# A sparse graph-attention layer: weight loads ordered behind attention's first work, degrees and target rows kept in a small table, the second sort's scatters spaced wider

## The chip, the cores and the metric

The kernel runs on one core of a Trainium2 chip. The metric is the device time of one execution in microseconds (us). Before the change three runs took 1833.16, 1834.15 and 1836.34 us; the median is 1834.15 us.

## The reference

The inputs are x and h_target (4096 nodes, 512 features each), an adjacency matrix adj (4096 x 4096 integers, about 0.4% of them nonzero, the diagonal always set), a node mask that is all ones, and weights in float32. The layer is masked attention with 8 heads of 64, a feed-forward part with hidden size 2048, two residuals and a last normalisation:

```
hs = layer_norm(x);  ht = layer_norm(h_target)
q = (ht @ Wq + bq) / sqrt(64);  k = hs @ Wk + bk;  v = hs @ Wv + bv
logits = einsum('thd,shd->hts', q, k);  logits = where(adj != 0, logits, -1e30)
ctx  = einsum('hts,shd->thd', softmax(logits), v)
ht   = layer_norm(ht + ctx @ Wo + bo)
out  = _layernorm(x + ht + gelu(ht @ W1) @ W2)
```

A row of adj has some 10 to 40 nonzeros (its degree), so most of the 4096 x 4096 logits are never needed.

## The kernel before

The kernel does the attention sparsely. It goes through these stages, which overlap.

**Lists.** For each of 32 tiles of 128 target rows, `edges` (L716) loads four quarters of adj (512 KB each, on SyncE's DMA queue, SP), takes the sign of each entry on ScalarE (L728), and finds the column numbers of the nonzeros with VectorE's maximum operations (L733 to L756). The candidates of each tile that go beyond the first 24 are kept by a write to DRAM, `rest_d` (L766, on SP); the buffer `gid` that this write reads has only one copy, so the next tile's L747 on VectorE waits until the write has landed. The result for a target row is a record: its degree (`DEG`, word 0), its own row number (`TGT`, word 1), two numbers for its first normalisation, and up to 40 column numbers.

**Sort.** The rows are sorted by degree, in two parts of 16 tiles, so that each tile of 128 sorted rows has a tight cap on its degree (`CAPS_A`, `CAPS_B`). `sort(part)` (L807) computes ranks and then writes the records to DRAM (`recs_d`) with 16 indirect scatters on GpSimd's queue (L853).

**Projections.** `project` (L864) goes through x in 16 groups of two tiles and computes k and v; `source` (L919) copies the two products out of PSUM on ScalarE (L931) and stores a tile's k|v rows (512 KB) to the DRAM table `kvd` by ScalarE's DMA queue (L935). A gather of k|v may name any source row, so the first gather has to wait until the last of these stores has landed.

**Attention.** Sorted tile by sorted tile, `attention` (L1164) processes segments of up to three neighbours per target row. GpSimd gathers the k|v rows by record (L966 within `issue`, L1055; 512 KB a gather, one slot of the buffer `ring` each; up to five segments ahead). VectorE multiplies by q and sums (L1217, L1222), ScalarE takes the exponential, and the values are weighted, two neighbours by VectorE (L1181) and the third by ScalarE in `by_scalar` (L1196; eight multiplications, L1201). TensorE adds the weighted values up, transposed, in PSUM (L1189). A tile's front (`front`, L982) gathers its h_target rows by `TGT` (L966), normalises them (L994 on VectorE, L995 on ScalarE), transposes (L999) and computes q (L1008). L994 takes a value of the last k|v copy, of the last segment's logits later on, as an operand, only in order to set its place in the order. `finish` (L1074) divides by the softmax's sum, applies Wo and the second normalisation.

**Feed-forward.** `feed` (L1310) handles one group of one or two tiles: hidden products (L1325), gelu (L1328), output products (L1334). Halfway it gathers the group's x rows into `xt` by `TGT` (L1352); `end` (L1276) adds, normalises and scatters the finished rows to `out` by `TGT` (L1302). W1 and W2 come in quarters. The first two are loaded early on SP, the last two (4 loads of 1 MB) by `weights` (L1436) on ScalarE's queue, into memory that the projections have used (`pools`, L1432).

**Buffers and checks.** A record lies in on-chip memory in one of 7 buffers `rec` (L977). It is read by the front, by the k|v gathers, in `finish`, and last by the x gather and the output scatter, so that its buffer comes free when the output scatter has landed. `verdict` (L1249), traced after the last tile, checks the softmax sums and the degrees. It reads the degrees of all rows back from `recs_d` by two DMAs on SP (L1259), one 4-byte word per row, into `degs`, and compares them with the caps on VectorE (L1262, L1265).

**Order.** The Python code weaves generators: `_weave` (L400) takes a step from the stream whose planned time is smallest, and each `yield` gives the planned time of the step. In the last weave there are four streams:

```
_weave((att, 0), (chain(feed(g) for g in range(len(GROUPS))), 0), (other_lists(), WAIT),
       (weights(), 0))
```

`weights` traces the third quarter at its planned time 10 and the fourth at 20. A segment of the first attention tile takes about 8 units of planned time. The traced order gives priorities. A planner then builds each engine's fixed instruction order: an instruction that is ready earlier in its model may go ahead of earlier traced ones. On the chip each engine and each DMA queue's issuing engine runs its instructions strictly in that order, so one that waits holds up everything behind it. Buffers and waits are derived from the tiles that instructions touch.

Of the kernel before, what the change touches and what calls it, by code (L numbers as in the profile page):

```python
# [443 lines left out]
def adj_resnorm_kernel(  # L444
# [88 lines left out]
    with tc.tile_pool(name="keep", bufs=1) as keep:  # L533
# [10 lines left out]
        cols = keep.tile([P, 5 * KC], F32, name="cols")  # L544
        s1c, b1c, s2c, b2c, bvc = (cols[:, i * KC:(i + 1) * KC] for i in range(5))
        sums = keep.tile([P, NT, H], F32, name="sums")
        degs = keep.tile([P, NT, 1], I32, name="degs")
        bad = keep.tile([P, 8], F32, name="bad")
        nc.vector.memset(bad, 0.0)

        with ExitStack() as late:
# [255 lines left out]
            def sort(part):  # L807
# [44 lines left out]
                for i in range(n):  # L852
                    ins = nc.gpsimd.indirect_dma_start(  # L853
                        out=recs_d[part][:, :],
                        out_offset=bass.IndirectOffsetOnAxis(ap=ranki[:, i:i + 1], axis=0),
                        in_=R[:, i, :], in_offset=None)

                    tc.declare_no_dep(ins.ins, group=f"scatter{part}", reason="other rows")
                    tc.add_to_no_dep_group(f"scatter{part}", ins.ins)
                    yield 1.3  # L860
                done.add(part)


            def project(order, t=None):  # L864
# [54 lines left out]
                def source(n, j):  # L919
                    g, hT = order[n], state[n][1]  # L920
                    if asked or moms:
                        kvr = sp.tile([P, 2 * D], F32, name="tq", bufs=3)
                    else:

                        kvr = ring[:, 8 + (n * G + j) % 3, :]
                    for half, w in enumerate((wk, wv)):
                        pkv = psi.tile([P, D], F32, name="pq", bufs=3)
                        for kc in range(KC):
                            nc.tensor.matmul(pkv, hT[:, kc, j * P:(j + 1) * P], w[:, kc, :],  # L929
                                             start=kc == 0, stop=kc == KC - 1)  # L930
                        nc.scalar.copy(kvr[:, half * D:(half + 1) * D], pkv)  # L931
                    if n >= 14:
                        latest[:] = [kvr[:, 0:1]]
                    r0 = 1 + (g * G + j) * P
                    nc.scalar.dma_start(kvd[r0:r0 + P, :], kvr)  # L935
                    return 7.8

                with tc.manual_schedule(engines={mybir.EngineType.DVE}):
# [21 lines left out]
                        yield cost  # L960


            recs, tqs, h2Ts, done, ready, latest = {}, {}, {}, set(), [], []

            def gather(dst, table, idx):
                nc.gpsimd.indirect_dma_start(  # L966
# [3 lines left out]
            def prefetch(i):  # L970
                if i >= NT or i in recs:
                    return
                r0 = TILES[i][0]
                part = 1 if r0 >= PARTS[1][0] * P else 0
                assert part in done
                r0 -= PARTS[part][0] * P
                rec = sp.tile([P, E0 + MAXE], I32, name="rec", bufs=7)  # L977

                nc.gpsimd.dma_start(rec[:, :RW], recs_d[part][r0:r0 + P, :])
                recs[i] = rec  # L980

            def front(i, idle=0):  # L982


                rec = recs[i]
                tq = sp.tile([P, 2 * D], F32, name="tq", bufs=3)
                t = tq[:, :D]
                gather(t, h_target, rec[:, TGT:TGT + 1])
                for _ in range(1 + idle):
                    yield  # L990


                m = rec[:, RST:RST + 2].bitcast(F32)
                nc.vector.scalar_tensor_tensor(m, m, latest[-1], m, op0=ALU.bypass, op1=ALU.max)  # L994
                nc.scalar.activation(t, t, AF.Identity, bias=m[:, 1:2], scale=m[:, 0:1])  # L995
                yield
                pt = ps.tile([P, KC, P], F32, name="t", bufs=2)
                for kc in range(KC):
                    nc.tensor.transpose(pt[:, kc, :], t[:, kc * P:(kc + 1) * P], ident)  # L999
                hT = tq[:, D:].rearrange("p (c t) -> p c t", c=KC)  # L1000
                for kc in range(KC):
                    nc.scalar.activation(hT[:, kc, :], pt[:, kc, :], AF.Identity,  # L1002
                                         bias=b1r[:, kc:kc + 1], scale=s1c[:, kc:kc + 1])
                yield
                yield
                pq = ps.tile([P, D], F32, name="t", bufs=2)
                for kc in range(KC):
# [156 lines left out]
            def attention():  # L1164
# [31 lines left out]
                def by_scalar(kv, lg):  # L1196
                    pa = sp.tile([P, H], F32, name="pa")
                    nc.scalar.activation(pa, lg[:, S - 1, :], AF.Exp)  # L1198
                    for hd in range(H):
                        v = kv[:, S - 1, D + hd * HD:D + (hd + 1) * HD]  # L1200
                        nc.scalar.mul(v, v, pa[:, hd:hd + 1])  # L1201

                request(0)
                yield 0.0
# [44 lines left out]
            def verdict():  # L1249
# [5 lines left out]
                nc.vector.scalar_tensor_tensor(ok, sf, SUM_HI, ok, op0=ALU.is_lt, op1=ALU.mult)  # L1255
                nc.vector.tensor_reduce(bad[:, 3:4], ok, AX.X, ALU.min)
                nc.vector.tensor_scalar(bad[:, 3:4], bad[:, 3:4], 1.0, None, op0=ALU.not_equal)
                for (i0, n), rec in zip(PARTS, recs_d):
                    nc.sync.dma_start(degs[:, i0:i0 + n, :], rec.rearrange("(n p) w -> p n w", p=P)  # L1259
                                      [:, :, DEG:DEG + 1])  # L1260
                for i, cap in enumerate(CAPS_A + CAPS_B):
                    nc.vector.tensor_scalar(over[:, i:i + 1], degs[:, i, :], float(cap),  # L1262
                                            None, op0=ALU.is_gt)
                nc.vector.tensor_reduce(bad[:, 4:5], over, AX.X, ALU.max)
                nc.vector.tensor_scalar(over, degs[:, :, 0], 1.0, None, op0=ALU.is_lt)  # L1265
                nc.vector.tensor_reduce(bad[:, 5:6], over, AX.X, ALU.max)
                b1 = sp.tile([P, 1], BF16, name="b1", bufs=1)
                nc.vector.tensor_reduce(b1, bad, AX.X, ALU.max)
# [7 lines left out]
            def end(group, xs, po):  # L1276
# [24 lines left out]
                for j, i in enumerate(group):  # L1301
                    ins = nc.gpsimd.indirect_dma_start(  # L1302
                        out=out[:, :], out_offset=bass.IndirectOffsetOnAxis(
                            ap=recs[i][:, TGT:TGT + 1], axis=0),
                        in_=xs[j], in_offset=None)

                    tc.declare_no_dep(ins.ins, group="out", reason="other rows")
                    tc.add_to_no_dep_group("out", ins.ins)

            def feed(g):  # L1310
# [34 lines left out]
                for f0 in range(fb, FC, fb):  # L1345
# [3 lines left out]
                    if f0 == FC // 2:  # L1349
                        for i in group:  # L1350
                            xt = sp.tile([P, D], F32, name="xt")
                            gather(xt, x, recs[i][:, TGT:TGT + 1])  # L1352
                            xs.append(xt)
                    if f0 == fb:

# [80 lines left out]
            def weights():  # L1436


                for q, pool in enumerate(pools):
                    yield 10.0  # L1440
                    load_quarter(pool, q + 2, nc.scalar)

            def other_lists():
                for cost in ed:
# [41 lines left out]
```

## Time and profile before

| | |
|---|---|
| runs | 1833.16, 1834.15, 1836.34 us; median 1834.15 |
| profiled execution | span 1826.4 us from the first to the last instruction, 22937 instructions |
| TensorE (PE) busy | 1687.8 us, 92% |
| VectorE (DVE) busy | 1432.2 us, 78% |
| ScalarE (ACT) busy | 1222.0 us, 67% |
| GpSimd (POOL) busy | 973.8 us, 53% |
| DMA | 463.27 MB, mean 254 GB/s |
| mean granted TensorE clock | 0.963 of full speed |

The profile describes one execution. Its time outside the span is not given; the median of the runs lies 7.75 us above the span. Line numbers (L966) are those of the kernel's file. "Idle before" is the time in which an engine had nothing running just before an instruction; the arrow names what ended it. SPq and ACTq are the DMA issues of SyncE and ScalarE. A share of busy time is a mean over stages with different limits, so the stretches of time count for more than the totals.

### The profile page before, as it was taken

The numbers are of one execution on the slowest core, as the hardware profiler recorded it, in microseconds if no ns is written. First come the engines' busy times: TensorE is split into PE (matmuls) and PEld (weight loads), VectorE is DVE, ScalarE is ACT, GpSimd is POOL, SyncE is SP. The second block draws the span as 40 slices with busy tenths as digits, with TensorE's granted clock in tenths as the row PEclk, the third lists the DMA queues.
The fourth block names the chain that finished last, engine by engine and source line by source line (L and its number), as shares of the span: only waits on it lengthen the run. The fifth ranks groups of instructions, "written<-read, shape, count | busy, mean of one in ns | idle before, by whom it ended". The sixth has DMA issues, their size and how long they took to land. (4 is left out here: it accounts for less than half of the span.)

```text
span 1826.4 us, 22937 instructions
## 1 busy us (share of the span) xinstructions
PE 1687.8 (92%) x7030; PEld 1102.5 (60%) x7030; DVE 1432.2 (78%) x2628; ACT 1222.0 (67%) x3119; POOL 973.8 (53%) x834
## 2 busy tenths in 40 slices
PE   7989983698998989999998998999999999999997
PEld 3444431475666656767676666666666666667664
DVE  6999855999999838786967998999888797988200
ACT  5767634487987637676767777778777676787311
POOL 1000143746566477657567778877574656763101
PEclk9999996698999999999998999999999999999999
DMA  9999958988896648767769978787776767674000
GB/s 354 373 395 365 341 192 309 360 291 312 286 331 231 209 121 312 245 239 260 261 211 308 308 245 302 252 296 265 240 272 222 256 214 262 228 269 159 17 7 25
DMA packets 144396, 463.27 MB, mean 254 GB/s; under 512 B 20628, under 2 KB 25800, under 8 KB 144264
## 3 DMA queue, kind: packets, MB, share of 16 engines
q0 software_dynamic: 96656, 342.64, 54.7%
q1 hardware_dynamic: 39792, 96.00, 14.6%
q10 hardware_dynamic: 7816, 23.08, 3.3%
q8 instruction: 58, 0.95, 0.2%
q14 instruction: 74, 0.61, 0.1%
HBM read 430.76 MB, written 30.89 MB: 253 GB/s over the span
## 5 line engine op out<-in xcount | busy, mean ns | idle before, releaser
L966 POOL DMA_INDIRECT kv<-kvd,rec x603 | 751.4, 1246 | 376.2 <-PE cps L1189 161.4
L1334 PE MATMUL po<-w,gt 128*128 128x512 f32 x1024 | 464.9, 597 | 6.2 <-ACT gt L1328 6.0
L1325 PE MATMUL pf<-h2T,w 128*128 128x256 f32 (+1 forms) x2176 | 464.8, 367 | 0.3 <-ACT h2T L1143 0.3
L1325 PEld LDWEIGHTS pf<-h2T,w 128*128 128x128 f32 x2176 | 388.1, 190 | 64.6 <-issue 20.7
L1217 DVE TENSOR_TENSOR kv<-kv,tq 128x1536 f32<-128x1536 f32 (+2 forms) x211 | 351.7, 1675 | 88.1 <-DMA kv<-kvd,rec 82.9
L1201 ACT ACTIVATE kv<-kv,pa 128x64 f32<-128x64 f32 x1520 | 391.2, 336 | 4.4
L1222 DVE TENSOR_REDUCE lg<-kv 128x24 f32<-128x1536 f32 (+2 forms) x211 | 350.0, 1666 | 1.0 <-ACT pa L1198 0.2
L1189 PE MATMUL cps<-ident,kv 128*128 128x128 f32 x2008 | 269.0, 283 | 53.4 <-issue 23.5
L1189 PEld LDWEIGHTS cps<-ident,kv 128*128 128x128 f32 x2008 | 243.3, 147 | 122.4 <-issue 68.9
L1334 PEld LDWEIGHTS po<-w,gt 128*128 128x128 f32 x1024 | 188.6, 192 | 202.4 <-issue 195.5
L1181 DVE TENSOR_TENSOR kv<-kv,p 128x1024 f32<-128x1024 f32 (+1 forms) x211 | 250.9, 1193 | 23.8 <-ACT p L1226 20.3
L687 POOL TENSOR_TENSOR n_rs<-n_ve,mhalf 128x2 f32<-128x2 f32 (+2 forms) x51 | 46.4, 909 | 336.9 <-DVE n_ve L680 177.7
L728 ACT ACTIVATE kv<-kv 128x1024 uint8<-128x1024 int32 x128 | 134.8, 1054 | 77.1 <-DMA kv<-in_adj_dram 43.3
L1328 ACT ACTIVATE gt<-pf 128x512 f32<-128x512 f32 x128 | 76.3, 597 | 99.2 <-PE pf L1325 87.8
L1328 ACT ACT_TABLE_LOAD x103 | 132.1, 1283 | 1.6
L1008 PE MATMUL t<-wq,tq 128*128 128x512 f32 x256 | 122.2, 621 | 11.0 <-ACT tq L1002 7.8
L929 PE MATMUL pq<-wk,h2T 128*128 128x512 f32 x256 | 124.4, 630 | 7.2 <-ACT tq L931 3.6
L735 DVE MAX8 cand<-kv 128x8 uint16<-128x103 uint16 (+1 forms) x640 | 130.0, 252 | 0.5
L1226 ACT ACTIVATE p<-lg 128x24 f32<-128x24 f32 (+2 forms) x179 | 39.2, 219 | 128.8 <-DVE lg L1222 114.1
L1112 PE MATMUL t<-wo,rb 128*128 128x512 f32 x256 | 116.5, 597 | 0.0
L929 PE MATMUL pq<-wv,h2T 128*128 128x512 f32 x256 | 115.2, 593 | 0.8 <-ACT tq L931 0.8
L929 PEld LDWEIGHTS pq<-wk,h2T 128*128 128x128 f32 x256 | 50.3, 203 | 72.9 <-issue 59.1
(158 smaller groups left out, 1578.4 us busy)
## 6 DMA issues: line engine op xcount, KB each, us to landing
kv<-in_adj_dram SPq DMA_DIRECT2D x128, 512.0 KB
kvd<-tq ACTq DMA_DIRECT2D x24, 512.0 KB
kv<-kvd,rec POOLq DMA_INDIRECT x603
kv<-in_L_gnn_h_target_dram SPq DMA_DIRECT2D x32, 256.0 KB
kv<-in_x_dram SPq DMA_DIRECT2D x15, 512.0 KB
rest_d<-gid SPq DMA_DIRECT2D x32, 160.0 KB
w<-in_L_gnn_W_dram SPq DMA_DIRECT2D x4, 1024.0 KB
kvd<-kv ACTq DMA_DIRECT2D x8, 512.0 KB
```

Of the source, the lines that this page charges most:

```text
L728: nc.scalar.activation(sg, a, AF.Sign, accum_out=dpart[:, i, h:h + 1])
L735: nc.vector.max(cand[:, h * SQ + s, :], wd[:, w0:w1])
L929: nc.tensor.matmul(pkv, hT[:, kc, j * P:(j + 1) * P], w[:, kc, :], start=kc == 0, stop=kc == KC - 1)
L966: nc.gpsimd.indirect_dma_start(out=dst, out_offset=None, in_=table[:, :], in_offset=bass.IndirectOffsetOnAxis(ap=idx, axis=0))
L1181: nc.vector.tensor_tensor(v4, v4, p[:, j0:j0 + m, :].unsqueeze(3) .to_broadcast([P, m, H, HD]), ALU.mult)
L1189: nc.tensor.matmul(cps[:, c, :], kv[:, j, D + c * P:D + (c + 1) * P], ident, is_transpose=True, start=j0 + j == 0 and c == 0, stop=j0 + n ...
L1201: nc.scalar.mul(v, v, pa[:, hd:hd + 1])
L1217: nc.vector.tensor_tensor(kv[:, :n, :D], kv[:, :n, :D], tq[:, :D].unsqueeze(1).to_broadcast([P, n, D]), ALU.mult)
L1222: nc.vector.tensor_reduce(lg[:, :n, :], kv[:, :n, :D].rearrange("p j (h d) -> p j h d", h=H), AX.X, ALU.add)
L1325: nc.tensor.matmul(pf[:, k, :], w1[(f0 + k) // KC][:, kc, (f0 + k) % KC * P:((f0 + k) % KC + 1) * P], h2T[:, kc, :w], start=kc == 0, stop= ...
L1328: nc.scalar.activation(gt, pf, AF.Gelu_apprx_tanh)
L1334: nc.tensor.matmul(po[j], gt[:, k, j * P:(j + 1) * P], w2[(f0 + k) // KC][:, (f0 + k) % KC, :], start=False, stop=f0 + k == FC - 1, skip_g ...
```

## The change

There are four edits.

1. `newest` always holds the last k|v store on ScalarE's queue or, once attention has started, the last multiplication of `by_scalar`. `weights` traces its loads inside `tc.issue_after(newest[-1])`: each load is issued on ScalarE after that instruction. It isn't made to wait until that instruction has finished.
2. The array `degs` (one word per row and tile) becomes `tags` (two words, degree and target row). `front` copies the two words out of the record by VectorE. The x gather and the output scatter take the row number from `tags`; `verdict` takes the degrees from it, and its two DMAs are gone. `rec` gets 6 buffers.
3. `TILES` gives the caps in sorted order in `verdict`, since `tags` is in the order in which attention takes the tiles.
4. The scatters of the second sort are 3.0 units of planned time apart, not 1.3; the first sort's stay at 1.3.

```diff
-        degs = keep.tile([P, NT, 1], I32, name="degs")
+        tags = keep.tile([P, NT, 2], I32, name="tags")
...
-                    yield 1.3
+                    yield 3.0 if part else 1.3
                 done.add(part)
...
-                    nc.scalar.dma_start(kvd[r0:r0 + P, :], kvr)
+                    newest[:] = [nc.scalar.dma_start(kvd[r0:r0 + P, :], kvr).ins]
...
-                rec = sp.tile([P, E0 + MAXE], I32, name="rec", bufs=7)
+                rec = sp.tile([P, E0 + MAXE], I32, name="rec", bufs=6)
...
+                nc.vector.tensor_copy(tags[:, i, :], rec[:, DEG:TGT + 1])
                 m = rec[:, RST:RST + 2].bitcast(F32)
...
                     for hd in range(H):
                         v = kv[:, S - 1, D + hd * HD:D + (hd + 1) * HD]
-                        nc.scalar.mul(v, v, pa[:, hd:hd + 1])
+                        newest[:] = [nc.scalar.mul(v, v, pa[:, hd:hd + 1]).ins]
...
-                for (i0, n), rec in zip(PARTS, recs_d):
-                    nc.sync.dma_start(degs[:, i0:i0 + n, :], rec.rearrange("(n p) w -> p n w", p=P)
-                                      [:, :, DEG:DEG + 1])
-                for i, cap in enumerate(CAPS_A + CAPS_B):
-                    nc.vector.tensor_scalar(over[:, i:i + 1], degs[:, i, :], float(cap),
+                for i, (_, cap) in enumerate(TILES):
+                    nc.vector.tensor_scalar(over[:, i:i + 1], tags[:, i, DEG:DEG + 1], float(cap),
                                             None, op0=ALU.is_gt)
...
-                nc.vector.tensor_scalar(over, degs[:, :, 0], 1.0, None, op0=ALU.is_lt)
+                nc.vector.tensor_scalar(over, tags[:, :, DEG], 1.0, None, op0=ALU.is_lt)
...
-                            ap=recs[i][:, TGT:TGT + 1], axis=0),
+                            ap=tags[:, i, TGT:TGT + 1], axis=0),
...
-                            gather(xt, x, recs[i][:, TGT:TGT + 1])
+                            gather(xt, x, tags[:, i, TGT:TGT + 1])
...
                 for q, pool in enumerate(pools):
                     yield 10.0
-                    load_quarter(pool, q + 2, nc.scalar)
+                    with tc.issue_after(newest[-1]):
+                        load_quarter(pool, q + 2, nc.scalar)
```

More of the change, by code (lines that the diff above doesn't have):

```diff
@@ L960, in project @@
                         yield cost
-            recs, tqs, h2Ts, done, ready, latest = {}, {}, {}, set(), [], []
+            recs, tqs, h2Ts, done, ready, latest, newest = {}, {}, {}, set(), [], [], []
             def gather(dst, table, idx):
```

## The prediction

> **What bounds the kernel now.** I read the page's busy times first, then the busy time by stretch, then the engines' timelines where the stretches show a hole, then the waits. The chain that ended last covers only the last 11 us (output normalise, flag, final scatter) and says nothing of the body.
>
> Busy time by stretch (columns: stretch; PE, PEld, DVE, ACT, POOL busy; granted clock; DMA share; GB/s):
>
> ```profile
> 300.00:310.00 10.00, 0.00 (x0) 0.00 (x0) 0.00 (x0) 2.30 (x4) 6.57 (x7) 0.59 0.96 357
> 310.00:320.00 10.00, 0.00 (x0) 0.00 (x0) 7.78 (x12) 4.53 (x14) 7.90 (x6) 0.50 1.02 409
> 320.00:330.00 10.00, 6.58 (x29) 5.78 (x30) 9.86 (x10) 4.67 (x20) 8.08 (x7) 0.50 1.03 419
> ...
> 480.00:500.00 20.00, 19.72 (x91) 13.67 (x89) 20.00 (x41) 19.57 (x44) 11.48 (x9) 1.00 0.86 301
> ...
> 660.00:680.00 20.00, 14.02 (x58) 9.00 (x57) 6.35 (x6) 7.99 (x21) 12.76 (x14) 0.85 0.45 114
> ...
> 1760.00:1780.00 20.00, 20.00 (x72) 13.36 (x71) 0.00 (x0) 1.79 (x3) 0.00 (x0) 1.00 0.00 1
> ```
>
> Three regimes: about 252 to 312 us nothing is full (the hand-over from projections to attention); about 320 to 560 us DVE is full; from 700 us PE is full, and after attention ends (1692 us) PE alone works off FFN until 1813 us. So the end is PE's work plus PE's idle time: about 50 us idle in 220 to 360 us, 58 us after 400 us. An edit pays if it removes PE idle time, or shifts the DVE-full stretch earlier.
>
> The hand-over, from the timelines (start, length, what, idle before and its releaser):
>
> ```profile
> 262.73 0.38 SPq L1259 DMA_DIRECT2D degs<-rec  x1
> 263.19 14.29 SPq L766 DMA_DIRECT2D rest_d<-gid  x2
> ```
> ```profile
> 273.89 0.49 DVE L747 SCALAR_TENSOR_TENSOR gid<-kv,segoff 128x320 f32<-128x320 uint16 x1 [18.32 <-DMA rest_d<-gid]
> ...
> 312.21 1.76 DVE L1217 TENSOR_TENSOR kv<-kv,tq 128x1536 f32<-128x1536 f32 x1 [12.30 <-DMA kv<-kvd,rec]
> ```
> ```profile
> 263.31 0.58 ACT L931 COPY kv<-pq 128x512 f32<-128x512 f32 x1 [10.50 <-DMA rec<-R,kv]
> ...
> 278.06 0.81 ACT L995 ACTIVATE tq<-tq,rec 128x512 f32<-128x512 f32 x1 [11.32 <-DVE rec L994]
> ...
> 289.78 0.39 ACTq L586 DMA_DIRECT2D w<-in_L_gnn_W_dram  x1
> ...
> 290.38 0.34 ACTq L935 DMA_DIRECT2D kvd<-kv  x1
> ```
> ```profile
> 301.58 0.94 POOL L966 DMA_INDIRECT kv<-kvd,rec  x1 [23.95 <-DMA w<-in_L_gnn_W_dram]
> ```
>
> SP's degree read waits for the first sort's scatters and holds the finished rest_d write (its data was ready at 251.7) behind it; DVE waits 18.32 us for that write; ACT waits for DVE; PE's transposes and last k|v product wait for ACT; the last k|v store goes out behind a weight load and lands 11.2 us later, when the first gather starts.
>
> **What the Trainium skill says.** "DMA: Bandwidth & Descriptors", Anatomy of one DMA: about 2.0 us fixed plus bytes at 436 GB/s. Here tile 8's h_target gather (256 KB, estimate 2.6) took 2.55 us from the end of its issue (581.79) to ACT's start (584.34): agrees. For 512 KB I estimate 3.2. Same page, Queues, rings and completion order: each DMA engine goes round-robin over the queues that have work. That fits a store of 11.2 us beside 2 MB of weights. "TensorE: Matmul & The Clock Gate", What's actually happening: an idle PE window halves the clock. Here the clock is 0.50 at 310 to 330, and eight 128x512 products took 5.61 us after a gap, 3.60 otherwise.
>
> **The change part by part.**
>
> *1. Degree reads gone from SP, weight loads behind ACT's by_scalar muls.* The planner traces weight loads at its times 10 and 20, when the newest ACT instructions are the muls of attention segments 0 and 1: they go behind those, not merely behind the store. I rebuild the hand-over. Unchanged: scatters end 261.5, POOL's record loads start 263.30. rest_d goes out at 251.8 and lands by 254.7, so DVE loses no 18.32 us. The first record, issued by 263.9, landed 270.24 beside 2 MB of weights and the degrees; alone I take 266.1 (POOL issues five loads until 266.03). The two h_target gathers end their issue at 267.1 and 268.3, land (+2.55) by 270.9; ACT L995 is done at 271.7, the transposes take 0.9, the last k|v product starts 272.6 (before 280.69). At full clock 2 x 3.6 = 7.2: ends 279.8; copy 0.58: store at 280.4 (before 290.38). Landing 0.34 + 3.2: first gather 284.0 (before 301.58). Third gather's issue ends two spacings of 1.245 and 0.94 later, 287.4; +3.2 = 290.6 for the first product on DVE (before 312.21): -21.6. ACT's 10.50 goes too, under the same path.
> What is given back: the same 4.19 MB of weights now lands among the first gathers, where DMA is already at 1.02. At 410 GB/s that is 10.2 us: at most +10.2, at least 0 (gathers run up to five segments ahead). With two queues alternating, gathers get about 205 GB/s for 20 us against a need of 1.57 MB per 4.7 us of DVE (335): 2.6 MB short, five slots, about the lead there is by then. I take +4. Net -17.6, kept to the end since DVE is full behind it. The first FFN group starts at 374 and needs these quarters at about 390: 70 us of cover; a slip past it would stall PE one for one. The second degree read (666.73) held nothing behind it: 0.
>
> *2. Record buffers 7 to 6, late users read the table.* Now a record waits for an output scatter:
>
> ```profile
> 571.26 2.03 POOL L1302 DMA_INDIRECT out_dram<-xt,rec  x1 [0.31 <-issue]
> 575.85 0.58 POOL L979 DMA_DIRECT2D rec<-rec  x1 [2.56 <-DMA out_dram<-xt,rec]
> 576.74 1.13 POOL L966 DMA_INDIRECT xt<-in_x_dram,rec  x1 [0.30 <-issue]
> ```
> ```profile
> POOL rec L979 <- DMA out_dram<-xt,rec: 24.5, 11, 4.8
> ```
>
> The x gather right behind needs the xt buffer that the same scatter frees. With the record load gone ahead, it waits in its place: of the 24.5 us I credit 0 (bounds: -8, the dip at 960 to 980, to +3). But tile 8's record came only 4 us before its h_target gather; ACT then waited 6.26 us and PE 4.92 at 585. A record freed at its tile's last softmax step (tile 2: 392.5) comes long before: -4 (0 to -4.9). Six buffers suffice: loads run two tiles ahead, and tile i-6 is then finished.
>
> *3. Copies to the table.* 32 on DVE; the nearest row, a 128x16 cast, took 0.15 us: 4.8 us in all. Hidden after 560 (DVE 15.6 of 20); six fall where DVE is full: +0.9. If all were exposed, +4.8. Each stands just before L994 on DVE and needs a record that L994 needs too: no new stall. The verdict's ops keep their number.
>
> *4. Second sort's scatters at 3.0.* Today the 16 run in 28 us (635.6 to 663.6) with four k|v gathers among them; DVE then waits 5.59, 6.78 and 11.76 us for gathers, ACT's gelu comes late behind it, and PE idles 5.98 us at 669.5. The same 16 x 1.27 = 20 us of POOL spread over 48 planner units leave room: -4 (-6 to +4 if POOL gets tight). Part two's first record is loaded at 940, so 27 units more is covered.
>
> Sum: -17.6 - 4 + 0.9 - 4 = -24.7. The profiled span 1826.4 becomes 1801.7. Runs lie 7.75 us above that span (median 1834.15), which I keep: **1809.5 us**. A new order may shift PE idle elsewhere by 6 us either way.
>
> **Rivals.** *A, the transfer ramp takes over:* weights cost their whole 10.2 us where DMA stands at 1.02, and parts 2 and 4 give nothing: -21.6 + 10.2 + 0.9 = -10.5, 1823.7. For it: DMA share above 1 for 30 us. Against: gathers already stop for free slots at 327. *B, no change:* the full DVE stretch has its list work moved behind attention instead of before it, so that the 21.6 us come back as later PE idle: about 1833. Against: SP's early release lets adjacency loads and lists run in DVE's holes. *C, slower:* the table is one buffer written by DVE and read by DMA; if a copy for tile i waits for earlier readers of other columns, each of 25 copies after the first scatters (487) waits for a scatter's landing, 2.0 to 4.8 us; at 2.5 that is 62 - 24.7 = +38, 1872. It decides the sign above 1 us per copy. Against: the kv ring is also one buffer, and its slots are written and read without such waits. *That the weights don't move* would leave the record path alone, about -10, inside A.
>
> **How the numbers follow.** Chances: mine 0.63 (own range 1795 to 1820), A 0.20, B 0.06, C 0.11. Within 0.2% (3.7 us, what a measurement tells from no change) is B: faster 0.83, same 0.06, slower 0.11. Range 1795 to 1830: mine with the lower bounds of parts 2 and 4 at one end, A with +6 of new order at the other; beyond lie B, C and a bit of mine.
>
> **What would show it.** DVE's 18.32 wait on rest_d gone; first gather near 284, first L1217 near 291; weight loads on ACT at about 297 and 303, with gather waits of 4 us in total there; rec waits on out_dram near 0 and xt waits near 24; PE's 4.92 and 5.98 gone; L1217 waits at 650 to 690 below half of 24. Wrong if the record lands no earlier than 270, the store still takes 8 us, or DVE waits ahead of the copies.

## The result and the profile after

The changed kernel takes 1826.55 us (median of 20 runs, 1820.38 to 1832.14), the kernel before, measured beside it, 1832.72 us (20 runs). The ratio is 0.9964 with a 95% interval of 0.9952 to 0.9976: 6.2 us faster. The forecast was 1809.5 us, 24.7 us faster. The sign and the range held, the size was a quarter of what was forecast.

The profiled execution spans 1818.6 us (before 1826.4). In every run of which both are on record the time lies 1.7 to 2.5 us above the span. So the 7.75 us of before are not time outside the span: its profiled execution was shorter than the median, as that of the change was (1820.38 us, the shortest of 20). In the changed file the copy to the table stands at L993 and all later lines are one further (L994 is L995, L1189 is L1190, L1217 is L1218), until `verdict`'s shorter text makes them two fewer (L1302 is L1300, L1334 is L1332).

The hand-over in the timeline of the changed kernel (start, length, engine, line, what it does, idle before and its releaser):

```profile
253.18 0.33 SPq L766 DMA_DIRECT2D rest_d<-gid  x1
...
266.95 0.17 DVE L993 COPY tags<-rec 128x2 int32<-128x2 int32 x1 [12.14 <-DMA rec<-rec]
...
268.73 1.06 ACT L728 ACTIVATE kv<-kv 128x1024 uint8<-128x1024 int32 x1 [12.22 <-DVE cand L735]
...
270.87 5.16 PE L929 MATMUL pq<-wk,h2T 128*128 128x512 f32 x8 [5.15 <-ACT h2T L914]
...
294.62 0.33 ACTq L935 DMA_DIRECT2D kvd<-kv  x1
...
301.63 0.94 POOL L966 DMA_INDIRECT kv<-kvd,rec  x1 [26.97 <-DMA kvd<-kv]
...
312.74 1.76 DVE L1218 TENSOR_TENSOR kv<-kv,tq 128x1536 f32<-128x1536 f32 x1 [2.02 <-DMA kv<-kvd,rec]
...
318.69 0.39 ACTq L586 DMA_DIRECT2D w<-in_L_gnn_W_dram  x1
```

SP is free: `rest_d` goes out at 253.18, and the wait of 18.32 us on it is gone. In its place VectorE stands for 12.14 us before the first copy to the table. The planner put this copy ahead of list work that was ready; ScalarE waits 12.22 us for that list work, and PE behind it. The last store goes out at 294.62, 4.2 us later than before. The first gather, which waits for it, starts 7.0 us after that, with adjacency loads and no weights beside the store. So the first gather starts at 301.63 and the first product at 312.74 (before 301.58 and 312.21): the hand-over ends where it did. The first of the weight loads now stands at 318.69, behind the multiplications of `by_scalar`.

The same stretches as shown of before (columns: stretch; PE, PEld, DVE, ACT, POOL busy; granted clock; DMA share; GB/s):

```profile
310.00:320.00 10.00, 0.15 (x1) 0.15 (x2) 6.43 (x9) 3.84 (x12) 7.87 (x8) 0.50 1.03 415
320.00:330.00 10.00, 5.49 (x24) 4.69 (x24) 10.00 (x11) 3.57 (x15) 5.71 (x6) 0.50 1.03 406
480.00:500.00 20.00, 20.00 (x104) 15.15 (x103) 20.00 (x45) 16.83 (x40) 10.19 (x9) 1.00 0.84 279
660.00:680.00 20.00, 16.31 (x61) 9.74 (x60) 6.51 (x7) 7.04 (x18) 15.74 (x16) 0.91 0.64 204
```

VectorE's hole at 660 to 680 is as it was (6.51 busy, before 6.35). From the view of waits (engine and line, what it waited for: us in total, times, longest):

```profile
DVE tags L993 <- DMA rec<-rec: 48.1, 13, 12.1
...
POOL xt L966 <- DMA out_dram<-xt,tags: 25.3, 12, 7.0
```

GpSimd's waits of 24.5 us for output scatters have left the record loads and stand before the x gathers. VectorE has 48.1 us of waits for records that weren't there.

Where the time went is read from TensorE, since the end is its work plus its idle time. Busy time by long stretches (the same columns), first before, then of the changed kernel:

```profile
240.00:560.00 320.00, 258.51 (x1118) 171.95 (x1117) 274.06 (x627) 219.09 (x565) 189.82 (x154) 0.88 0.82 294
560.00:1100.00 540.00, 511.31 (x2330) 354.52 (x2329) 421.86 (x471) 367.76 (x1013) 363.84 (x311) 0.97 0.73 246
1100.00:1700.00 600.00, 589.25 (x2543) 400.32 (x2544) 517.42 (x602) 450.32 (x1201) 388.31 (x322) 1.00 0.72 244
```
```profile
240.00:560.00 320.00, 257.60 (x1111) 170.51 (x1110) 278.03 (x648) 216.72 (x559) 186.68 (x159) 0.87 0.83 293
560.00:1100.00 540.00, 515.87 (x2383) 360.50 (x2382) 434.36 (x487) 379.06 (x1047) 376.99 (x318) 0.98 0.76 256
1100.00:1700.00 600.00, 592.50 (x2536) 399.54 (x2535) 507.30 (x605) 443.96 (x1182) 381.69 (x312) 0.99 0.72 237
```

PE is idle 62.4, 24.1 and 7.5 us in them; before it was 61.5, 28.7 and 10.8. The gain lies in the second and third stretch. In the first, where the hand-over is, there is none.

### The profile page after: what moved, and what is told of

The parts are those of the page before. It is cut to its first block, busy times and chain, and to the rows that moved or that the text cites. A ratio compares the mean times of both kernels' runs of the same rounds, so it can differ in the third digit from the quotient of the medians.

```text
span 1818.6 us, 22965 instructions
## 1 busy us (share of the span) xinstructions
PE 1686.6 (93%) x7030; PEld 1100.9 (61%) x7030; DVE 1435.0 (79%) x2660; ACT 1221.5 (67%) x3119; POOL 976.5 (54%) x834
## 5 line engine op out<-in xcount | busy, mean ns | idle before, releaser
L1332 PE MATMUL po<-w,gt 128*128 128x512 f32 x1024 | 466.3, 598 | 6.6 <-ACT gt L1326 6.3
L1218 DVE TENSOR_TENSOR kv<-kv,tq 128x1536 f32<-128x1536 f32 (+2 forms) x211 | 352.0, 1678 | 51.0 <-DMA kv<-kvd,rec 48.4
L1332 PEld LDWEIGHTS po<-w,gt 128*128 128x128 f32 x1024 | 188.9, 192 | 203.2 <-issue 195.2
L1190 PE MATMUL cps<-ident,kv 128*128 128x128 f32 x2008 | 267.5, 281 | 45.3 <-issue 22.7
L1190 PEld LDWEIGHTS cps<-ident,kv 128*128 128x128 f32 x2008 | 240.9, 146 | 112.7 <-issue 69.8
L687 POOL TENSOR_TENSOR n_rs<-n_ve,mhalf 128x2 f32<-128x2 f32 (+2 forms) x51 | 50.1, 983 | 329.8 <-DVE n_ve L680 154.5
L1009 PE MATMUL t<-wq,tq 128*128 128x512 f32 x256 | 117.4, 602 | 5.0 <-ACT tq L1003 4.3
```

The source lines that it names most:

```text
L1190: nc.tensor.matmul(cps[:, c, :], kv[:, j, D + c * P:D + (c + 1) * P], ident, is_transpose=True, start=j0 + j == 0 and c == 0, stop=j0 + n ...
L1218: nc.vector.tensor_tensor(kv[:, :n, :D], kv[:, :n, :D], tq[:, :D].unsqueeze(1).to_broadcast([P, n, D]), ALU.mult)
L1332: nc.tensor.matmul(po[j], gt[:, k, j * P:(j + 1) * P], w2[(f0 + k) // KC][:, (f0 + k) % KC, :], start=False, stop=f0 + k == FC - 1, skip_g ...
```

## The experiments

All ratios are to the kernel before, run on the same chip; 0.001 is 1.8 us.

### The parts alone

First theory: the prediction's parts hold, and the copy's wait of 12.14 us at the hand-over hides the gain. Rival: it is elsewhere. `copy_late` is the whole change with each copy placed behind the first use of the record on VectorE, which needs the record anyway:

```diff
-                nc.vector.tensor_copy(tags[:, i, :], rec[:, DEG:TGT + 1])
                 m = rec[:, RST:RST + 2].bitcast(F32)
-                nc.vector.scalar_tensor_tensor(m, m, latest[-1], m, op0=ALU.bypass, op1=ALU.max)
+                ins = nc.vector.scalar_tensor_tensor(m, m, latest[-1], m, op0=ALU.bypass, op1=ALU.max)
+                with tc.issue_after(ins.ins):
+                    nc.vector.tensor_copy(tags[:, i, :], rec[:, DEG:TGT + 1])
```

> The changed kernel with one edit: each copy to the table is ordered behind L994 of its tile on VectorE, so that it no longer stands ahead of list work. Theory 1 (the copy for tile 0, which VectorE reaches 12.14 us before its record has landed, holds the list work, ScalarE's copies and the last k|v store): the 12.14 us wait disappears, the first k|v gather comes at 284 to 290 us and not at 301.6, the first L1217 product at 291 to 297 and not at 312.7, and the kernel takes 1810 us or less, at least 10 us below the changed kernel. Theory 2 (the weights among the first gathers took the gain): the hand-over moves as well, but VectorE loses 10 us or more to gathers before 360 us, and the time stays within 4 us of the changed kernel. Theory 3 (VectorE's full stretch gives all of it back, whatever the hand-over does): gathers without large waits, time within 4 us of the changed kernel.

Measured: 0.9922 (0.9898 to 0.9947), 1816.93 us. It beats both kernels. But its hand-over is only 3 us earlier (store 291.87, first gather 298.67, first product 310.20): 7.7 us by the ratios (0.9964 - 0.9922) were gained over the change, and in none of the three ways that were expected.

`order_only` is the kernel before with the weight loads inside `tc.issue_after(newest[-1])` and nothing else.

> The kernel before with the weight loads' order alone. SP's degree read and VectorE's 18 us wait stay. Theory 1: ScalarE's 10.50 us wait is gone and the last store lands in 4 to 7 us and not 11, so that the first gather is 4 to 8 us earlier; weights among the first gathers give 4 us back: 1826 to 1834 us. Theory 2: they give 10 us back: 1836 us or more.

Measured: 0.9976 (0.9966 to 0.9987), 4.4 us. The first gather is 2.7 us earlier (298.93, before 301.58), 6.9 us after the last store's issue.

`table_only` has the table, the copies and six record buffers, with `load_quarter` not ordered and the scatters 1.3 apart. The degree reads, which the prediction counts in its part 1, are gone in it too.

> The kernel before with the table alone (copies, 6 record buffers, no degree reads); the weight loads are not ordered and the second sort's scatters are 1.3 apart. Theory 1: the copies' wait of about 12 us stays, SP's wait is gone, and the weights again go out ahead of the last store: about as the kernel before, 1829 to 1836 us. Theory 2: without weights among the first gathers it is clearly faster than the changed kernel, 1823 us or less.

Measured: 0.9992 (0.9974 to 1.001).

`spacing_only` is the kernel before with one line changed:

```diff
-                    yield 1.3
+                    yield 3.0 if part else 1.3
                 done.add(part)
```

> The kernel before with the second sort's scatters 3.0 apart and nothing else. As forecast: VectorE's gather waits at 650 to 690 us (24 us) fall below half, PE's 5.98 us idle at 669 goes, and 4 us are gained: about 1829 us. Rival: PE has enough feed-forward work there, nothing is gained: within 2 us of the kernel before.

Measured: 0.9996 (0.9978 to 1.0013). The sixteen scatters start from 642.6 to 674.8 us in this run, 635.4 to 668.9 with the whole change, 635.6 to 663.6 before: 32 and 33.5 us in place of 28, where 48 units of planned time were asked. A planned time sets a priority; an instruction that is ready goes when its engine is free. VectorE's gather waits that were to fall below half are 7.95 and 12.46 us in this run (at 672 and 691 us; 24.1 us in all before).

The three parts together make -4.4 - 1.5 - 0.7 = -6.6 us, the whole change -6.2 (-6.6 by its ratio). Each part is known to 2 or 3 us only, so that they add up proves little. And every edit lets the planner build the order anew: no run changes one thing on the chip alone.

### Does the hand-over reach the end?

Second theory: it does, but adjacency loads now compete with the last store as the weights did. `late_hold` is `copy_late` with SP's adjacency loads queued behind a small read of the last row of `kvd`, which waits for the store:

```diff
+            hold.append(nc.sync.dma_start(last_row, kvd[N:N + 1, 0:8]).ins)
...
-                nc.sync.dma_start(a, adj[i * P:(i + 1) * P, h * QW:(h + 1) * QW])
+                with tc.issue_after(hold[0]):
+                    nc.sync.dma_start(a, adj[i * P:(i + 1) * P, h * QW:(h + 1) * QW])
```

(Loads traced before the read keep their place.)

> copy_late with SyncE's adjacency loads for the second part's lists held until the last k|v store has landed (a small read of its last row, behind which they queue). Theory: these loads, let go early since the degree read is gone, are what makes records, h_target rows, the last store (6.8 us) and the first gathers (7 us) land late: with them held, the store lands in under 4.5 us, the first gather comes at 290 us or earlier and the first product before 298 (310.2 in copy_late). For the time: if the hand-over's end sets it, 8 to 12 us less than copy_late; if VectorE's total work to 560 us sets it, the lists lost to the hole cost as much, and the time is within 4 us or longer.

Measured: 0.9921 (0.9896 to 0.9945). Timeline of this kernel (columns as above; its lines are four further):

```profile
283.21 0.33 ACTq L939 DMA_DIRECT2D kvd<-kv  x1
...
285.85 0.28 SPq L1448 DMA_DIRECT2D last_row<-kvd  x1
...
286.11 0.69 DVE L1019 SCALAR_TENSOR_TENSOR tq<-t,bqr 128x512 f32<-128x512 f32 x1 [15.37 <-PE t L1014]
286.78 0.94 POOL L970 DMA_INDIRECT kv<-kvd,rec  x1 [10.95 <-DMA last_row<-kvd]
...
295.43 1.76 DVE L1223 TENSOR_TENSOR kv<-kv,tq 128x1536 f32<-128x1536 f32 x1 [2.27 <-DMA kv<-kvd,rec]
```

This is the hand-over that the prediction rebuilt, within 5 us: the read that waits for the store is issued 2.6 us after it, the first gather starts 3.6 us after it, and the first product starts 15 us ahead of `copy_late`'s. The end does not move. At the end of tile 0 (L1079 of before) 8.7 us of the 15 are left, at tile 2 none: 388.89 against 389.14. VectorE had stood for 15.37 us while lists waited, and did them afterwards: from 240 to 560 us it is busy for 279.1 us, and for 280.0 in `copy_late`. So the run shows that a hand-over bought with standing still is worth nothing; one that comes early with the lists done as well was not made.

`late_no_w` is `copy_late` without the loads of the last two quarters of W1 and W2; the first two quarters stand in for them, so that their 4 MB are never moved.

```diff
-                    with tc.issue_after(newest[-1]):
-                        load_quarter(pool, q + 2, nc.scalar)
+                    w1.append(w1[q])
+                    w2.append(w2[q])
```

> copy_late without the last four weight loads: the third and fourth quarters of W1 and W2 are not loaded, the first two quarters stand in for them, everything else is kept. It prices the weights among the first gathers. Theory 2: the stretch from the first L1217 product to the end of tile 1 (52 us there, 42.6 in the kernel before) falls to 43 us or less, and the time falls by 6 to 10 us. Rival: VectorE's list work fills the same stretch and the time stays within 3 us of copy_late.

Measured: 0.9927 (0.9899 to 0.9955). From the first product to the end of tile 1 it takes 43.0 us, as before the change (42.6), where the change takes 51.8. So the weights do cost their 9 us there, and the end is not told from that of `copy_late`.

`late_w_later` puts them at planned times 30 and 45, in place of 10 and 20.

> copy_late with the weight loads traced at planned times 30 and 45, not 10 and 20, so that they go out at about 343 and 358 us, behind the ramp of the first gathers. Theory 2: some 4 us of the ramp's price are saved, 1812 us; the first feed-forward group still finds its weights. Rival: the price moves with them, since the gathers fill the DMA engines until 360 us: within 3 us of copy_late.

Measured: 0.9957 (0.9938 to 0.9975); its interval meets that of `copy_late`, so it tells only that later is no gain.

### Is VectorE's work the bound?

Third theory, from rival B: VectorE's total work up to 560 us sets the end. `late_more_lists` adds two maxima to each quarter of tiles 21 to 31, `late_44` four:

```diff
                         nc.vector.max(cand[:, h * SQ + s, :], wd[:, w0:w1])
+                        if i >= NA + FILL and s < 2:
+                            nc.vector.max(again, wd[:, w0:w1])
```

> The changed kernel with late copies (1816.93 us, 0.9922 of before), with two MAX8 of 103 columns (about 0.25 us each) added to each quarter of the adjacency of tiles 21 to 31: 88 instructions, 22 us more work on VectorE, between 260 and 560 us, nothing else changed. Theory, that VectorE's amount of work up to about 560 us sets the end and the hand-over's own end does not: 12 to 22 us over the kernel with late copies, 0.998 to 1.004 of before, and TensorE's idle time from 240 to 560 us up by as much. Rival, that the bound there is the DMA queues or TensorE: less than 5 us over, 0.992 to 0.995.

> The changed kernel with late copies and four MAX8 of 103 columns added to each quarter of the adjacency of tiles 21 to 31: 176 instructions, 44 us more work on VectorE between 260 and about 620 us (22 us more did not move the end: 0.9915). Theory, that VectorE's own waits at 600 to 690 us (34 us in the kernel with late copies, 28 with the 22 us added) are a slack that absorbs what is late before: 44 us use it up, and the time is 10 to 22 us over the kernel with late copies, 0.998 to 1.004. Rival, that VectorE's work in this stretch does not matter to the end at all: under 5 us over, 0.991 to 0.995.

Measured: 0.9915 (0.9888 to 0.9943) and 0.9934 (0.9914 to 0.9954). Neither is told from `copy_late`: the theory fell. But the work was less than the 22 and 44 us that were reckoned from one maximum's length: VectorE's busy time grows by 11.8 and 26.5 us (1447.1 and 1461.8 against 1435.3), since maxima that follow each other overlap (five take 0.93 us, one 0.26). In the profile of `late_44` tiles 7, 8 and 9 end (start of L1079 of before) at:

```profile
610.67 0.29 DVE L1084 SCALAR_TENSOR_TENSOR p<-rec,p 128x136 f32<-128x136 int32 x1
655.31 0.28 DVE L1084 SCALAR_TENSOR_TENSOR p<-rec,p 128x144 f32<-128x144 int32 x1
699.52 0.32 DVE L1084 SCALAR_TENSOR_TENSOR p<-rec,p 128x152 f32<-128x152 int32 x1
```

In `copy_late` they end at 589.89, 633.99 and 696.56. VectorE is 21 us late at tile 8 and 3 us at tile 9, mostly because it waits less there: its idle time between the two ends is 29.8 us in `copy_late` and 18.3 in `late_44`. A lead goes there too: `table_late` (below) ends tile 8 at 626.45, 7.5 us ahead of `copy_late`, and tile 9 at 695.77, 0.8 us ahead. A lateness of more than these 30 us was not made.

Fourth theory: from tile 9 on VectorE's lateness counts. `late_work_mid` adds six maxima over 512 columns to the softmax's end of tiles 9 to 14, `late_work_end` to tiles 17 to 22:

```diff
-                nc.vector.reciprocal(ri, ri)
+                ins = nc.vector.reciprocal(ri, ri)
+                if 9 <= i <= 14:
+                    for _ in range(6):
+                        with tc.issue_after(ins.ins):
+                            ins = nc.vector.max(again, bqr)
```

> The changed kernel with late copies and six MAX8 of 512 columns (an estimated 0.7 us each, from the row of 0.48 us at 320) added on VectorE in the end of the softmax of each of the tiles 9 to 14, behind the reciprocal: 36 instructions, about 25 us more work between 700 and 940 us. 44 us in the lists before tile 8 moved the end by nothing. Theory, that VectorE's waits at tiles 8 to 9 are a slack for what lies before them alone, and that from tile 9 on its lateness reaches the end: 12 to 25 us over the kernel with late copies, 0.999 to 1.006. Rival, that TensorE's backlog covers VectorE's lateness everywhere: under 4 us over, 0.991 to 0.9945.

> The same 36 MAX8 in the tiles 17 to 22 instead (1120 to 1320 us), where TensorE is 99% busy in the kernel with late copies. Theory, that there only TensorE counts: under 4 us over the kernel with late copies, 0.991 to 0.9945. Rival, that VectorE's lateness reaches the end there: 12 to 25 us over, 0.999 to 1.006.

Measured: 0.9903 (0.9873 to 0.9933) and 0.9943 (0.9923 to 0.9962), with VectorE busy for 23.1 and 19.6 us more. The first is the rival's; the second lies at the edge of the band of under 4 us that was expected there. In none of the three stretches do 20 to 27 us more work on VectorE reach the end at their price.

That VectorE's lateness does not count is not shown by this, for the work of `late_work_mid` did not make it late: tile 14 ends at 937.39, 3.2 us after `copy_late`'s 934.21, since the maxima ran where VectorE had waited. Other kernels are late from tile 9 on and end late: `table_only`, `late_first` and `copy_pool` (below) end tile 10 some 10, 14 and 10 us after `copy_late`, and their profiled executions 15, 17 and 15 us after it.

### What does move it: the records and the copies

`late_old_recs` is `copy_late` with x gathers and output scatters indexed from the records again, in seven buffers. The copies stay, of the degree alone:

```diff
-                rec = sp.tile([P, E0 + MAXE], I32, name="rec", bufs=6)
+                rec = sp.tile([P, E0 + MAXE], I32, name="rec", bufs=7)
...
-                            ap=tags[:, i, TGT:TGT + 1], axis=0),
+                            ap=recs[i][:, TGT:TGT + 1], axis=0),
...
-                            gather(xt, x, tags[:, i, TGT:TGT + 1])
+                            gather(xt, x, recs[i][:, TGT:TGT + 1])
```

> The kernel with late copies, with the x gathers and the output scatters indexed from the records again, in seven record buffers (the copies stay, for the degrees alone): record loads wait for the scatters as before the change, some 24 us in all. Theory, that the gain comes from records loaded early, with the h_target gather ahead of the next tile's k|v gathers (the step of 11 us between tiles 14 and 15): 8 to 12 us over the kernel with late copies, 0.9965 to 0.999, and the step gone. Rival, that the gain comes from the order of weights and other turns of the planner: under 3 us over, 0.9915 to 0.9945.

Measured: 1.0012 (0.9998 to 1.0026), 1833.57 us. With this edit everything is given back: 1.0012 - 0.9922 = 0.009, some 16 us. Part of that need not be the records': the run still has the weights' order, and is 0.0036 above `order_only`. Waits of this kernel on GpSimd, 560 to 1750 us:

```profile
POOL rec L979 <- DMA out_dram<-xt,rec: 21.5, 10, 4.7
```

Where a group's scatters free two record buffers at once, two records are loaded together, one of them late. With the table a record is loaded at the end of each tile, and earlier: that of tile 16 (the first tile is 0) at 940.05 before, at 942.17 in `late_old_recs`, at 751.03 in `copy_late`. What depends on it moves: the merging of long rows (`rest_of`, L779) in `late_old_recs` and in the changed kernel, in the view of the tile `gid` (duration min/median/max in ns, first and last start):

```profile
L779 DVE MAX8 rec<-gid x4: 485/486/494, 893.3 to 1024.6; 128x8 int32<-128x320 f32 x4
```
```profile
L779 DVE MAX8 rec<-gid x4: 494/495/495, 711.1 to 803.8; 128x8 int32<-128x320 f32 x4
```

VectorE's waits for k|v from 930 to 1030 us are 22.5 us before, 24.0 in `late_old_recs`, 11.3 after, 13.0 in `copy_late`. From the end of tile 14 to that of tile 15 it takes 88.6 us before, 77.8 after and 78.5 in `copy_late`; in `late_old_recs` it is 86.6 again. The two ends before and in `copy_late`:

```profile
937.90 0.36 DVE L1079 SCALAR_TENSOR_TENSOR p<-rec,p 128x192 f32<-128x192 int32 x1
1026.54 0.48 DVE L1079 SCALAR_TENSOR_TENSOR p<-rec,p 128x312 f32<-128x312 int32 x1
```
```profile
934.21 0.36 DVE L1081 SCALAR_TENSOR_TENSOR p<-rec,p 128x192 f32<-128x192 int32 x1
1012.71 0.48 DVE L1081 SCALAR_TENSOR_TENSOR p<-rec,p 128x312 f32<-128x312 int32 x1
```

Most of the difference between the two profiled executions arises here: it is 3.7 us at tile 14, 13.8 at tile 15, and 12.6 at the end of the spans. `late_old_recs` is behind `copy_late` by 5.9 us at tile 14, 14.0 at tile 15, 19.0 at tile 17 and 20.1 at the end.

`table_late` is `table_only` with late copies.

> The table of copies alone (weights and spacing as before), with each copy ordered behind the dense max of its tile. With the copies early the table was worth 1.5 us (0.9992). Theory, that the waits of the copies cost what the late copies gained in the whole change (some 8 us): 0.994 to 0.996, 1818 to 1825 us. Rival, that the late copies pay only where the weights are also out of the hand-over: within 2 us of the table alone, 0.998 to 1.0.

Measured: 0.9931 (0.9903 to 0.9958), more gain than either expectation had. The table with late copies is nearly the whole of `copy_late`; early copies take some 11 us of it away (0.9992).

`late_first` and `late_rest` split the copies: late for tiles 0 to 4 alone, and for tiles from 5 on alone.

```diff
+                if i > 4:
+                    nc.vector.tensor_copy(tags[:, i, :], rec[:, DEG:TGT + 1])
...
-                with tc.issue_after(ins.ins):
-                    nc.vector.tensor_copy(tags[:, i, :], rec[:, DEG:TGT + 1])
+                if i <= 4:
+                    with tc.issue_after(ins.ins):
+                        nc.vector.tensor_copy(tags[:, i, :], rec[:, DEG:TGT + 1])
```

(`late_rest` has the two conditions exchanged.)

> The whole change, with only the copies of tiles 0 to 4 ordered behind their dense max, so that the 12.14 us wait of the hand-over goes and the waits at 598 to 850 us stay. Theory, that the hand-over's waits do not reach the end: as the change itself, 0.9955 to 0.997. Rival, that the 12 us wait carried the cost: as with all copies late, 0.991 to 0.9935.

> The whole change, with only the copies of tiles from 5 on ordered behind their dense max: the 12.14 us wait of the hand-over stays, the waits of 3 to 6 us at 598 to 850 us go. Theory, that those later waits carry the cost: 0.991 to 0.9935. Rival, that the hand-over's wait carries it: 0.9955 to 0.997.

Measured: `late_rest` 0.9925 (0.9897 to 0.9953), the same as with all copies late, although the wait of the hand-over stays. `late_first` 0.9999 (0.998 to 1.0017), some 6 us slower than the change, which neither expectation had. The copies that stay early wait 26.4 us between 560 and 900 us in it, up to 9.1 us at once, against 22.2 and 5.9 in the change; tiles 7 to 10 lose 13.5 us on before (the change 9.3, `copy_late` 4.7). So it is the copies of tiles from 5 on that cost. Why `late_first` is worse than the change is not shown.

`copy_pool` is the change with its early copies on GpSimd (`nc.gpsimd.tensor_copy`).

> The change with its copies to the table on GpSimd, whose queue waits for the records anyway since the gathers are indexed by them, and nothing ordered late. Theory, that the copies cost because VectorE stands before them (48 us in 13 waits): 0.990 to 0.994, with no wait for a record on VectorE at the copies. Rival, that the order that the planner takes costs, whatever engine copies, or that GpSimd standing costs as much: 0.9955 to 1.0.

Measured: 1.0022 (1.001 to 1.0034), above the ranges of both. In the view of instruction groups of this kernel (busy, mean ns, then idle before):

```profile
L993 POOL COPY tags<-rec 128x2 int32<-128x2 int32 x32 | 16.8, 530 | 40.4 <-DMA rec<-rec 40.3
```

The waits went to GpSimd with the copies, where k|v gathers stand behind them. That GpSimd's queue waits for records anyway was no cover: the copy had been placed earlier than the gathers that need the same record.

`late_spread` is `copy_late` with each scatter of the second sort ordered behind the gather traced just before it.

```diff
+                    with tc.issue_after(gathered[-1]) if part else ExitStack():
                         ins = nc.gpsimd.indirect_dma_start(
                             out=recs_d[part][:, :],
```

> copy_late with each scatter of the second sort forced behind the gather traced before it, so that the 16 really stand apart in GpSimd's order (one or two, then gathers), which the wider planned distance did not do. As forecast for the spacing: VectorE's gather waits at 650 to 700 us (20 us in copy_late) fall below 10, and 3 to 5 us are gained. Rival: TensorE works through feed-forward products meanwhile, so that the waits go and the time stays within 2 us.

Measured: 0.9937 (0.9921 to 0.9954), with waits of 12.05, 2.93 and 1.03 us for gathers at 650 to 690: 16 us, not below 10. Scatters further apart are no gain here, and they were not what those waits hung on.

## Why the prediction was wrong in size

The failed step is "kept to the end since DVE is full behind it": it carried 17.6 of the 24.7 us. In the change the earlier hand-over did not even arise (first product at 312.74, before 312.21). Where it did, in `late_hold` (295.43), the kernel ended where `copy_late` did. That VectorE is full at 320 to 560 us was read correctly, but a full engine passes a gain on only if its work is less or its waits are fewer: in `late_hold` the lists that were left undone came afterwards, and the lead was gone at tile 2. And VectorE is not full further on. Between the ends of tiles 8 and 9 it is idle for 30 us, and there 18 of the 21 us went by which `late_44` was late, and nearly all of the 7.5 us by which `table_late` led. What the runs show in its place is a gain that comes with the table of target rows, where the forecast had 3 us (-4 + 0.9): 12.6 us with late copies, of which the early copies left 1.5. That the time fell inside the forecast range is luck, since no account of the forecast leads to it.

Term by term:

| term | forecast | measured |
|---|---|---|
| 1, weights and degrees at the hand-over | -17.6 | -4.4, the weights' order alone |
| 2 and 3, records and copies | -4 + 0.9 | -1.5 alone, as they are in the change (degree reads gone too) |
| 2 and 3 with late copies | | about -12.6 (degree reads gone too) |
| 4, spacing | -4 | -0.7 (-4 to +2.4) |
| sum | -24.7 | -6.6; the whole -6.2 |

*Part 1.* Right: DVE's wait of 18.32 us goes, the record's landing (issue 264.91, first use 266.95; I took 266.1), the weights' place behind `by_scalar`. Wrong: the store's landing of 3.5 us. The Trainium skill's price of one transfer ("DMA: Bandwidth & Descriptors", Anatomy of one DMA), from which I estimated 3.2 us for 512 KB, is fitted there to DMAs that GpSimd issues, and the store is ScalarE's. In `late_hold`, where little lands beside it, the store had landed 2.6 us after its issue, and the gather started at 3.6. In the change the gather started at 7.0: SP, no longer held, sent five adjacency loads from 285 us on. Nor does the round robin between queues by itself account for the 11.2 us of before, as I read it: the two weight loads stood in the store's own queue, one of them 0.6 us ahead of it, and adjacency loads came on SP's. From the end of the third gather's issue to the product it took 7.7 us, not 3.2. I had named the store as a sign against me ("still takes 8 us"), and took the weights for its only company.

*Part 3* was the worst of the small ones: "each stands just before L994 on DVE and needs a record that L994 needs too: no new stall". It is traced there; the planner placed it up to 12 us of waiting earlier, since it needs nothing but the record. That is the sign I had named last, "DVE waits ahead of the copies". It is worth 0.9964 - 0.9922 = 0.0042, 7.7 us, over eight times the +0.9. Most of it does not come from the longest wait.

*Part 2.* The x gathers' waits in the record loads' place are as foretold (25.3 us for 24). The price of early records was too small: I took the dip at 960 to 980 as the bound of -8 and credited tile 8 with -4. The measured gain, 12.6 us in `table_late` and up to 16 from `late_old_recs` to `copy_late`, comes mostly in that dip, between the ends of tiles 14 and 15, with records of later tiles loaded singly and long rows merged 200 us sooner.

*Part 4.* The waits at 650 to 690 are 7.96 and 6.06 us and no longer 5.59, 6.78 and 11.76, above the half that I named. In `copy_late`, the faster kernel, they are 7.90 and 11.72: these holes don't decide.

*Rivals.* A's number, 1823.7, is the nearest, and its ramp is real: the first product to tile 1 takes 9.2 us more. But `late_no_w` shows that this is not why the time is what it is. B had the right consequence, and half of the account: in `late_hold` the earlier hand-over comes back as B says, with the list work moved behind it. But that work does not set the end, since 26.5 us more of it did not show. C did not occur: no copy waits for a reader of the table, all 48.1 us are waits for records.

Open is how the early records make the step at tile 15. From `late_old_recs` to `copy_late` PE's idle time falls by 3.9, 5.7 and 6.6 us in the three long stretches (66.0, 28.4 and 12.9 against 62.1, 22.7 and 6.2), and PE's busy time by 7.2 us (1689.5 against 1682.3, at granted clocks of 0.963 and 0.965). Between the ends of tiles 14 and 15 it falls from 9.2 to 3.9 us (7.7 before). That the difference in VectorE's order arises at this step and stays to the end is seen; which wait the records shorten there was not isolated by a run.

## What to carry to other kernels

An engine that is full in one stretch proves nothing about the end: look for the next waits of that engine downstream, for here they absorbed both gains and losses, and test it by adding work to the stretch before counting on a gain there. See in the trace whether the added work made the engine late at all. A small instruction that needs only an early buffer can be put early by a planner and then holds an in-order engine until its DMA has landed (12.14 us at the longest); tie it behind an instruction that needs the same data (here worth more than the whole change). Freeing a buffer at its true last use paid here through what could be loaded early: the waits of 24.5 us that it took from the record loads came back as 25.3 us before the x gathers.

## What was not expected of the hardware

From the issue of one store of 512 KB to the start of the gather that waits for it, it took 11.2 us beside two weight loads and adjacency loads, 7.0 us beside adjacency loads, 3.6 us with neither. Where a transfer ends a stage, it is not enough to move the loads beside it: here the queue set free filled the place. A copy of 128x2 words takes 0.17 us on VectorE and 0.20 us on GpSimd (medians; GpSimd's mean of 0.53 us comes from single copies of up to 2.2 us).
